# A ring of three PSUM banks for the decays and side pieces of a Mamba stage, and a new layout of those pieces over its slots

## The chip, the cores and the metric

The kernel runs on one NeuronCore of a Trainium2 chip. The core has four engines that take instructions in order from queues of their own: TensorE (PE in the profile; its weight loads are listed as PEld), VectorE (DVE), ScalarE (ACT) and GpSimd (POOL). SyncE (SP) issues DMA transfers. The metric is the time of one execution on the device in microseconds. Three runs of the kernel before gave 2083.98, 2085.44 and 2085.51 us, so the median is 2085.44 us.

## The reference

The input is x of shape (8, 256, 128), which is 2048 tokens of 128 features. Six residual blocks follow each other, each on a layer-normalised x:

```python
x = x + 0.5 * cell(norm(x))        # six small attention nodes
x = x + attention(norm(x))         # 16 heads with rotary positions
x = x + 0.5 * cell(norm(x))
x = x + 0.5 * experts(norm(x))     # top 2 of 8 experts
x = x + mixer(norm(x))             # bidirectional Mamba and an FFT branch
x = x + 0.5 * experts(norm(x))
```

The change lies in the mixer and in the two expert blocks that share its stage. The mixer computes, for each batch entry with 256 channels `d`, 16 states `n` and 256 steps `l`:

```python
u     = silu(causal_conv(x_half))                 # once forward, once reversed
delta = softplus(W_dt @ dt + bias)
h[l]  = exp(delta[l] * A) * h[l-1] + delta[l] * B[l] * u[l]   # per (d, n)
y     = sum_n h[l] * C[l] + D * u
out   = (y_forward + y_reversed) * silu(z)
f     = abs(ifft2(silu(conv(fft2(x_half))))) * max(silu(z))   # then whitened
result = (out + (f - mean) / sqrt(var + 1e-5)) @ W_out
```

The factor `exp(delta * A)` is called the decay below. The reversed direction runs the scan from the last token to the first.

## The kernel before

The 2048 tokens are cut into 4 chunks of 512 (two batch entries each). The two cells and the attention come first and are not touched. One function, `experts_and_mixer`, then holds the first expert block, the mixer and the second expert block. Its scan is cut into 32 units per chunk, so 128 units in all. A unit holds 128 partitions and 2 x 512 elements.

**What a unit passes through.** `spread` (L1154) replicates rows over partitions with TensorE: a matmul pair writes `pU` (the factor delta x u, two PSUM banks), and another pair writes `pA` (delta). Each matmul contracts over one strip of 32 rows: the two of `pU` use one half of the four strips, and the two of `pA` of the unit two further on use the other half. ScalarE turns `pA` into the decay tile `dA` with two Exp instructions (L1177). `feed` (L1187) multiplies `pU` by B on VectorE in place. `scan` (L1198) is one VectorE instruction, after which GpSimd multiplies the result by C into `hc` (L1200). `sums` (L1211) adds two units' `hc` into the accumulator `py` on TensorE.

**What sets the order.** The code runs under a manual schedule of TensorE, VectorE, ScalarE and GpSimd: each of these queues keeps the order in which the program names the instructions. A loop over slots i issues scan(i), feed(i+1), the pieces listed for that slot in `before`, sums(i-3) in odd slots, the pieces listed in `after` (`last=True`), and last spread(i+2, i+4). A spread therefore makes `pU` two slots ahead and the decay four slots ahead. Slot s of chunk c is i = 32c + s; in a chunk's slots work of three chunks stands side by side.

**The pieces.** All that is not the scan is cut into pieces placed with `at(slot, function, ...)`: the convolutions (`convolve`), the gate, the silu calls, the low-rank step sizes (`ranks`, `steps`, `softplus`, `delta`), the DMA copies of B and C (`rows`), the FFT branch (`frequencies`, `pairs`, `mix`, `mirror`, `halves`, `over_channels`, `folds`, `over_tokens`, `magnitude`, `moments`, `whiten`), and the end (`weigh`, `join`, `output`). Most of the TensorE pieces write one PSUM bank that ScalarE then copies out. `mix` writes two SBUF tiles, `mix0` and `mix1`, which `mirror` reads on GpSimd in three instructions; there is one buffer of each.

**PSUM.** Of the eight banks, `pU` holds a ring of two tiles of two banks (four), `py` holds one, `pA` has one tile of two banks (tag "a"), and all pieces share one bank (tag "p", `bank` at L843). The transposes `pt` of the expert blocks use tag "a".

**Tables.** ScalarE loads a table (`ACT_TABLE_LOAD`) before silu, before Sqrt, and before it goes back to Exp and Ln. In a middle chunk silu runs in slots 20 and 32 and Sqrt in slot 45, so there are six loads per chunk.

Of the kernel before, what the change touches and what calls it, by code (L numbers as in the profile page):

```python
# [10 lines left out]
F32 = mybir.dt.float32  # L11
# [6 lines left out]
P = 128  # L18
# [780 lines left out]
def experts_and_mixer(nc, tc, ident, nhalf, x, cols, ins, w, given, store):  # L799
# [19 lines left out]
    with ExitStack() as ctx:  # L819
# [13 lines left out]
        for i in range(4):  # L833
            c = COLS["Dp"].start + i
            nc.gpsimd.tensor_scalar(w["D"][:, i, :], ident, cols[:, c : c + 1], None, ALU.mult)

        gots = [{} for _ in range(NCH)]
        before, after = {}, {}

# [1 line left out]
            (after if last else before).setdefault(slot, []).append(lambda: f(*a))  # L841

        def bank(shape):  # L843
            return ps.tile(shape, F32, tag="p", bufs=1, name="p")

# [85 lines left out]
        class Experts:  # L933
# [58 lines left out]
            def turn(self, n):  # L992
                if not 0 <= n < NCH * NT:
                    return
                both = self.tiles[n]["both"]
                pt = ps.tile([P, 4, P], F32, tag="a", bufs=1, name="pt")
                for k in range(4):
                    nc.tensor.transpose(pt[:, k, :], both[:, 0, k, :], ident)
                nc.scalar.copy(both[:, 1], pt)
# [71 lines left out]
        def exponentials():  # L1071

            nc.scalar.preload_act_table_set("natural_log_exp_and_others")
# [73 lines left out]
        def unit(n):  # L1147
            s = n % UNITS
            return n // UNITS, s // 16, s // 8 % 2, s // 2 % 4, s % 2
# [1 line left out]
        units = [{} for _ in range(NCH * UNITS)]  # L1151
        N = len(units)

        def spread(n, m):  # L1154

            todo = []
            if 0 <= n < N:
                ch, t, r, i, jp = unit(n)
                pU = ps.tile([P, 2, CT], F32, tag="u", name="pU")
                todo.append((pU, gots[ch]["du", t][:, r, :], i, 2 * (1 - jp)))  # L1160
                units[n]["dB"] = pU
            if 0 <= m < N:
                ch, t, r, i, jp = unit(m)
                pA = ps.tile([P, 2, CT], F32, tag="a", bufs=1, name="pA")
                todo.append((pA, gots[ch]["dl", t][:, r, :], i, 2 * jp))
            for jj in range(2):
                for dst, src, i, j in todo:
                    rs = slice(32 * (j + jj), 32 * (j + jj) + 32)
                    nc.tensor.matmul(  # L1169
                        dst[:, jj, :], w["sel"][rs, i, :], src[rs, :], start=True, stop=True  # L1170
                    )
            if 0 <= m < N:
                ch, t, r, i, jp = unit(m)
                dA = pool.tile([P, 2, CT], F32, tag="dA", name="dA", bufs=4)
                for jj in range(2):
                    j = 2 * jp + jj
                    nc.scalar.activation(  # L1177
                        dA[:, jj, :], pA[:, jj, :], AF.Exp, scale=A[:, r, t, i, j : j + 1]
                    )
                units[m]["dA"] = dA  # L1180

        def feed(n):
            if not 0 <= n < N:
# [144 lines left out]
            )  # L1328

        def magnitude(ch):  # L1330
            nc.scalar.activation(gots[ch]["mag"], gots[ch]["mag"], AF.Sqrt)
            exponentials()

        def largest(ch):
            got = gots[ch]
# [58 lines left out]
        def output(ch):  # L1394
            y = gots[ch]["sz"]
            po = bank([P, NT, D])
            for t in range(NT):
                for d in range(2):
                    nc.tensor.matmul(
                        po[:, t, :],  # L1400
                        y[:, d, t * P : (t + 1) * P],
                        w["outT"][:, d, :],
                        start=(d == 0),
                        stop=(d == 1),
                    )
            o = pool.tile([P, NT, D], F32, tag="sq", name="o", bufs=2)
            nc.scalar.copy(o, po)
            nc.gpsimd.tensor_tensor(x[ch], x[ch], o, ALU.add)

        def u_of(ch, t):  # L1410
            return lambda: (gots[ch]["u", t], None)
# [8 lines left out]
        def prepare(experts, c, k, *room):  # L1420

            at(k, experts.statistics, c)
            at(k + 1, experts.scale, c, *room)
            at(k + 1, experts.transpose, c, last=True)
            at(k + 2, experts.logits, c, last=True)
            at(k + 3, experts.gates, c, last=True)
# [31 lines left out]
        for n in range(NCH * NT + 2):  # L1458
            at(end + 1 + n, second.step, n)
        prepare(second, 2, end + 3, room)  # L1460
        prepare(second, 3, end + 8)

        at(-27, fetch, None)
        at(-27, fetch, 2)
# [13 lines left out]
        at(0, conv_weights, 3, 0, last=True)  # L1478
        at(1, conv_weights, 3, 1, last=True)

        for ch in range(NCH):

            o = (ch - 1) * UNITS
            if ch == 0:
                at(-8, ranks, ch, 1)
                at(-8, largest, ch)
                at(-7, steps, ch, 0, 0)
                at(-6, steps, ch, 0, 1)
                at(-6, exponentials)
                at(-6, softplus, ch)  # L1490
            else:
                for part, k in enumerate((-3, -2, 0, 0)):
                    at(o + k, normalize, ch, part)
                at(o + 1, features, ch)
                at(o + 2, convolve, ch, 1, 0)
                at(o + 12, convolve, ch, 1, 1)
                at(o + 16, convolve, ch, 0, 0)
                at(o + 17, gate, ch, 0, last=True)
                at(o + 18, convolve, ch, 0, 1)
                at(o + 19, gate, ch, 1, last=True)  # L1500
                at(o + 20, silu, u_of(ch, 0), u_of(ch, 1), sz_of(ch), sc_of(ch - 1, 0))
                at(o + 20, exponentials)
                at(o + 21, largest, ch)
                at(o + 21, ranks, ch, 0, last=True)
                at(o + 22, ranks, ch, 1)
                at(o + 23, steps, ch, 0, 0)
                at(o + 23, steps, ch, 0, 1, last=True)
                at(o + 24, softplus, ch)
            at(o + 24, rows, ch, 0, 0)
            at(o + (26 if ch == 0 else 25), delta, ch, 0, 0)  # L1510
            at(o + 26, delta, ch, 0, 1)
            at(o + 26, rows, ch, 0, 1)
            v = o + 4 * (ch == 0)
            at(v + 28, steps, ch, 1, 0)
            at(v + 29, steps, ch, 1, 1)
            at(v + 30, softplus, ch)
            at(v + 31, delta, ch, 1, 0)
            at(o + 32, rows, ch, 1, 0)
            at(v + 32, delta, ch, 1, 1)
            at(o + 34, rows, ch, 1, 1)  # L1520
            o += UNITS
            for t in range(2):
                at(o + 16 * t + 3, skip, ch, t, 0)
                at(o + 16 * t + 4, skip, ch, t, 1)
                at(o + 16 * t + 18, weigh, ch, t)
            at(o - (2 if ch == 0 else 1), frequencies, ch, 0)
            at(o - 1, frequencies, ch, 1, last=True)
            at(o + 10, pairs, ch, 1)
            at(o + 11, pairs, ch, 2)

            final = ch + 1 == NCH
            mixes = (12, 14, 16, 18) if final else (14, 24, 26, 29)
            for co, k in enumerate(mixes):
                at(o + k, mix, ch, co, 0, last=True)
                at(o + k + 1, mix, ch, co, 1, last=True)
                at(o + k + 2, mirror, ch, co)
            k = o + (21 if final else 32)
            at(k, silu, *(sc_of(ch, co) for co in range(0 if final else 1, 4)))
            at(k, exponentials)
            at(k + 1, halves, ch, 0)  # L1540
            at(k + 2, halves, ch, 1)
            for i in range(4):
                at(k + 3 + i, over_channels, ch, i // 2, i % 2, last=True)
                at(k + 5 + i, folds, ch, i // 2, i % 2)
            for i, j in enumerate((7, 8, 10, 11)):
                at(k + j, over_tokens, ch, i // 2, i % 2, last=True)
            at(k + 13, magnitude, ch)
            if final:
                k -= 3
            at(k + 14 + 3 * final, moments, ch, 0)  # L1550
            at(k + 15 + 2 * final, moments, ch, 1)
            at(k + 17 + final, whiten, ch, 0)
            at(k + 17 + final, whiten, ch, 1)
            at(k + 18 + final, join, ch)
            at(k + 21 - final, output, ch)
        engines = mybir.EngineType
        order = {engines.PE, engines.DVE, engines.Activation, engines.Pool}
        with tc.manual_schedule(engines=order):
            for i in range(min(before), max(*before, *after) + 1):
                scan(i)  # L1560
                feed(i + 1)
                for f in before.get(i, ()):
                    f()
                if i % 2:
                    sums(i - 3)
                for f in after.get(i, ()):
                    f()
                spread(i + 2, i + 4)


SHAPES = {
# [263 lines left out]
```

## Time and profile before

| what | us |
|---|---|
| median of three runs | 2085.44 |
| the profiled execution | 2090.59 |
| its span | 2088.8 |
| first matmul of the first expert block | 1330.1 |
| first unit's scan starts | 1433.5 |
| last unit's scan ends | 2013.4 |
| chunk 0, scan start to scan start | 147.8 |
| chunk 1 | 144.3 |
| chunk 2 | 142.0 |
| chunk 3, to the start of the last scan | 143.5 |
| after the last scan | 75.4 |
| one scan on VectorE | 2.29 |
| one feed on VectorE | 1.21 |
| one product by C on GpSimd | 2.36 |
| one decay Exp on ScalarE (two to a unit) | 0.68 |
| one table load on ScalarE | 1.28 |

Over the whole span TensorE is busy for 93%, VectorE for 75%, ScalarE for 55% and GpSimd for 39%. These are averages over stages with different limits. A timeline row gives the start, the duration, the engine, the line, the operation, the tiles (written <- read), the shapes and a count; the bracket behind it is the time that the engine was idle before it, and who ended that. The time from one scan to the next is that of a slot: 2.29 + 1.21 and a gap of about 0.04 give 3.54 us when nothing else is in the way, and 128 such slots would take 453 us.

### The profile page before, as it was taken

To read this page: it belongs to the slowest core of one execution; us is meant where nothing else is said; L and a number is where in the kernel's file an instruction comes from. 1 tells how busy PE (TensorE), PEld (TensorE's weight loads), DVE (VectorE), ACT (ScalarE), POOL (GpSimd) and SP (SyncE) were. 2 spreads that over 40 slices of the span, in tenths; PEclk is the share of its full clock that TensorE was granted. 3 is DMA by queue.
4 is the path that set the end of the run, shared out by engine and by line. 5 is a ranking of instruction groups with operands and counts; after the bars stand their busy time and mean duration, and the time that the engine had idled before them with its cause. 6 is when DMAs were issued, how large, how long until landed. Compare 5 with 4: busy or idle time off the path is not lost. (4 is left out here: it accounts for less than half of the span.)

```text
span 2088.8 us, 45123 instructions
## 1 busy us (share of the span) xinstructions
PE 1946.3 (93%) x17792; PEld 1127.5 (54%) x17792; DVE 1564.9 (75%) x2669; ACT 1151.7 (55%) x2202; POOL 812.7 (39%) x918
## 2 busy tenths in 40 slices
PE   6999999997999999999999998798888989889888
PEld 4666666654565665666666665453234433334445
DVE  5777777776878767677777777546987978888774
ACT  4777777752333323477777774445355555654544
POOL 3000001026666655100000003443767868778863
PEclk9999999998999999899999999899898999989899
DMA  4000000000000000000000000221000010010000
GB/s 143 3 3 3 3 3 3 3 2 1 2 2 2 2 2 2 2 3 3 3 3 3 3 3 2 107 68 24 11 21 21 1 24 18 4 38 1 1 1 21
DMA packets 21239, 29.23 MB, mean 14 GB/s; under 512 B 12506, under 2 KB 13914, under 8 KB 20260
## 3 DMA queue, kind: packets, MB, share of 16 engines
q1 hardware_dynamic: 20740, 26.15, 4.2%
q8 instruction: 141, 2.31, 0.5%
q14 instruction: 70, 0.57, 0.1%
q10 hardware_dynamic: 288, 0.20, 0.0%
HBM read 16.10 MB, written 1.05 MB: 8 GB/s over the span
## 5 line engine op out<-in xcount | busy, mean ns | idle before, releaser
L344 DVE TENSOR_REDUCE negmax<-sc 128x2 f32<-128x512 f32 x768 | 490.9, 682 | 158.0 <-PE sc L338 157.6
L349 ACT ACTIVATE ex<-sc 128x512 f32<-128x512 f32 x768 | 421.3, 609 | 198.2 <-PE sc L338 197.9
L338 PE MATMUL sc<-qk,qk 32*128 32x256 f32 x6144 | 472.8, 406 | 9.3 <-DVE negmax L344 8.5
L338 PEld LDWEIGHTS sc<-qk,qk 32*128 32x128 f32 x6144 | 296.5, 186 | 146.2 <-ACT ex L349 100.9
L1200 POOL TENSOR_TENSOR hc<-h,C 128x1024 f32<-128x1024 f32 x128 | 301.3, 2359 | 129.1 <-DVE h L1198 118.4
L1198 DVE TENSOR_TENSOR_SCAN h<-dA,pU 128x1024 f32<-128x1024 f32 x128 | 292.2, 2283 | 14.5 <-POOL hc L1200 2.2
L299 ACT ACTIVATE qk<-pp,w_bqk,head_rows 128x256 f32<-128x256 f32 x384 | 197.6, 573 | 74.3 <-PE pp L419 34.7
L85 POOL TENSOR_SCALAR ln_ve<-ln_mv 128x2 f32<-128x2 f32 (+1 forms) x56 | 13.3, 238 | 559.3 <-DVE ln_mv L83 552.0
L1177 ACT ACTIVATE dA<-pA,cols 128x512 f32<-128x512 f32 x256 | 162.1, 684 | 105.1 <-PE pA L1169 102.9
L1187 DVE TENSOR_TENSOR pU<-pU,B 128x1024 f32<-128x1024 f32 x128 | 155.7, 1216 | 76.5 <-PE pA L1169 72.4
L377 PE MATMUL pc<-ex,va 128*32 128x256 f32 x3072 | 206.0, 386 | 0.2 <-DVE y L442 0.2
L1169 PE MATMUL pU<-du,s_sel 32*128 32x512 f32 x512 | 173.2, 690 | 19.4 <-DVE h L1198 18.8
L621 ACT ACTIVATE ex<-sc 128x512 f32<-128x512 f32 x128 | 66.1, 602 | 204.8 <-PE sc L606 204.8
L1169 PE MATMUL pA<-dl,s_sel 32*128 32x512 f32 x512 | 159.3, 698 | 6.3 <-ACT dA L1177 6.3
L606 PE MATMUL sc<-rot,rot 32*128 32x256 f32 x2048 | 136.9, 392 | 1.9 <-POOL rot L589 1.9
L377 PEld LDWEIGHTS pc<-ex,va 128*32 128x32 f32 x3072 | 80.7, 109 | 96.6 <-issue 61.9
L606 PEld LDWEIGHTS sc<-rot,rot 32*128 32x128 f32 x2048 | 99.0, 186 | 37.1 <-issue 23.1
L198 POOL TENSOR_SCALAR w_bqk<-pb,head_rows 128x2 f32<-128x2 f32 x12 | 3.5, 316 | 295.8 <-DVE pb L195 288.9
L624 POOL TENSOR_TENSOR both<-ex 128x512 f32<-128x512 f32 x64 | 80.0, 1273 | 71.3 <-ACT ex L621 71.3
L1169 PEld LDWEIGHTS pU<-du,s_sel 32*128 32x128 f32 x512 | 49.3, 198 | 100.2 <-issue 81.5
L616 DVE TENSOR_REDUCE anegmax<-sc 128x2 f32<-128x512 f32 x128 | 79.5, 685 | 26.7 <-PE sc L606 26.7
L985 DVE TENSOR_TENSOR hid<-ph,gate 128x1024 f32<-128x1024 f32 x32 | 39.1, 1222 | 71.7 <-PE ph L980 68.7
(291 smaller groups left out, 3210.8 us busy)
## 6 DMA issues: line engine op xcount, KB each, us to landing
qk<-turned SPq DMA_DIRECT2D x768, 1.0 KB
s_fft<-s_fft SPq DMA_DIRECT2D x5, 1024.0 KB
du<-ab SPq DMA_DIRECT2D x16, 256.0 KB
B<-low SPq DMA_DIRECT2D x64, 32.0 KB
C<-low SPq DMA_DIRECT2D x64, 32.0 KB
x<-x SPq DMA_DIRECT2D x4, 256.0 KB
s_inK<-s_inK SPq DMA_DIRECT2D x1, 1024.0 KB
out<-x SPq DMA_DIRECT2D x4, 256.0 KB
```

The source lines that it names most:

```text
L299: nc.scalar.activation(t[:, g, :], pp, AF.Identity, scale=w["mask"][:, g : g + 1], bias=w["bqk"][:, c, i, g : g + 1],)
L338: nc.tensor.matmul(sc[:, t, :], lhs[:, t * P : (t + 1) * P], rhs, start=True, stop=True)
L344: nc.vector.tensor_reduce(sh[:, :, 4 * g + j], sc, AX.X, ALU.max, negate=True)
L349: nc.scalar.activation(ex, sc, AF.Exp, scale=FD**-0.5)
L377: nc.tensor.matmul(st["pc"][32 * j : 32 * j + 32, g, :], st[2][:, kt, 2 * j + g, :], st["ex", g, j][:, kt, :], start=(kt == 0), stop=(kt = ...
L606: nc.tensor.matmul(sc[j][:, t, :], lhs[r, part, t * P : (t + 1) * P] if part < 2 else sel[r, :], rhs[r, part, :] if part < 2 else st["nm"] ...
L624: nc.gpsimd.tensor_tensor(both, ex[:, :, 0], ex[:, :, 1], ALU.add)
L1169: nc.tensor.matmul(dst[:, jj, :], w["sel"][rs, i, :], src[rs, :], start=True, stop=True)
L1177: nc.scalar.activation(dA[:, jj, :], pA[:, jj, :], AF.Exp, scale=A[:, r, t, i, j : j + 1])
L1187: nc.vector.tensor_tensor(dB, dB, bcast(gots[ch]["B", r], 2), ALU.mult)
L1198: nc.vector.tensor_tensor_scan(hf, af, bf, 0.0, ALU.mult, ALU.add)
L1200: nc.gpsimd.tensor_tensor(hc, h, bcast(gots[ch]["C", r], 2), ALU.mult)
```

## The change

All of it lies in `experts_and_mixer`.

- **PSUM.** Tag "a" is gone. `bank` becomes a ring of three single banks, from which the pieces, the transposes `pt` and the decays are allocated in program order. A unit's decay takes two of these banks, one for each half, instead of one tile of two.
- **`spread(n, *ms)`** makes one `pU` and the decays of none, one or two units. Its matmuls are issued in the order pU half 0, first decay half 0, pU half 1, first decay half 1, second decay half 0, second decay half 1.
- **Bursts.** Seven slots (12, 26, 44, 58, 76, 90 and 114 of 0 to 127), those in which the silu calls now stand, are marked. The spread of such a slot b makes no decay, nor does that of b+1; those of b+2, b+3 and b+4 make two, one and two.
- **`magnitude`** takes the root as exp(log(x + 1e-30) / 2), two ScalarE passes, with no table load of its own.
- **`output`** is split: the addition to x is a piece `add` with a slot of its own.
- **The layout.** The slots of nearly all pieces change. Silu goes to slots 12 (u and z) and 26 (the FFT branch), convolutions and gates to slots 2 to 10, `ranks` and `steps` to 15 to 17, the `mix` pieces of chunks 0 to 2 to 13, 14, 18 and 20 to 24, their `over_channels` to 30 to 33, and in chunks 0 and 1 `over_tokens` to 36, 37, 43 and 44 (slots 4, 5, 11 and 12 of the next chunk) and `magnitude` to 51 (slot 19 of the next). In the last chunk the FFT branch ends in slot 129 instead of 132. The preparation of the fourth chunk for the second expert block starts three slots earlier.

The diff, cut to its core:

```diff
+        tiny = pool.tile([P, 1], F32, name="tiny")
+        nc.gpsimd.memset(tiny, 1e-30)
...
         def bank(shape):
-            return ps.tile(shape, F32, tag="p", bufs=1, name="p")
+            return ps.tile(shape, F32, tag="p", bufs=3, name="p")
...
-                pt = ps.tile([P, 4, P], F32, tag="a", bufs=1, name="pt")
+                pt = bank([P, 4, P])
...
-        def spread(n, m):
+        def spread(n, *ms):
             todo = []
             if 0 <= n < N:
                 ch, t, r, i, jp = unit(n)
                 pU = ps.tile([P, 2, CT], F32, tag="u", name="pU")
-                todo.append((pU, gots[ch]["du", t][:, r, :], i, 2 * (1 - jp)))
+                for jj in range(2):
+                    todo.append((jj, pU[:, jj, :], gots[ch]["du", t][:, r, :], i, 2 * (1 - jp) + jj))
                 units[n]["dB"] = pU
-            if 0 <= m < N:
-                ch, t, r, i, jp = unit(m)
-                pA = ps.tile([P, 2, CT], F32, tag="a", bufs=1, name="pA")
-                todo.append((pA, gots[ch]["dl", t][:, r, :], i, 2 * jp))
...
+            ms = [m for m in ms if 0 <= m < N]
+            decays = []
+            for k, m in enumerate(ms):
                 ch, t, r, i, jp = unit(m)
                 dA = pool.tile([P, 2, CT], F32, tag="dA", name="dA", bufs=4)
+                units[m]["dA"] = dA
                 for jj in range(2):
+                    pA = bank([P, CT])
+                    todo.append((2 * k + jj, pA, gots[ch]["dl", t][:, r, :], i, 2 * jp + jj))
+                    decays.append((dA[:, jj, :], pA, A[:, r, t, i, 2 * jp + jj : 2 * jp + jj + 1]))
+            for _, dst, src, i, j in sorted(todo, key=lambda v: v[0]):
+                rs = slice(32 * j, 32 * j + 32)
+                nc.tensor.matmul(dst, w["sel"][rs, i, :], src[rs, :], start=True, stop=True)
+            for dA, pA, rate in decays:
+                nc.scalar.activation(dA, pA, AF.Exp, scale=rate)
...
         def magnitude(ch):
-            nc.scalar.activation(gots[ch]["mag"], gots[ch]["mag"], AF.Sqrt)
-            exponentials()
+            mag = gots[ch]["mag"]
+            nc.scalar.activation(mag, mag, AF.Ln, bias=tiny)
+            nc.scalar.activation(mag, mag, AF.Exp, scale=0.5)
...
-                at(o + 12, convolve, ch, 1, 1)
-                at(o + 16, convolve, ch, 0, 0)
-                at(o + 17, gate, ch, 0, last=True)
-                at(o + 18, convolve, ch, 0, 1)
-                at(o + 19, gate, ch, 1, last=True)
-                at(o + 20, silu, u_of(ch, 0), u_of(ch, 1), sz_of(ch), sc_of(ch - 1, 0))
+                at(o + 6, convolve, ch, 1, 1)
+                at(o + 7, gate, ch, 0)
+                at(o + 8, convolve, ch, 0, 0)
+                at(o + 9, gate, ch, 1)
+                at(o + 10, convolve, ch, 0, 1)
+                at(o + 12, silu, u_of(ch, 1), u_of(ch, 0), sz_of(ch))
...
-            mixes = (12, 14, 16, 18) if final else (14, 24, 26, 29)
-            for co, k in enumerate(mixes):
-                at(o + k, mix, ch, co, 0, last=True)
-                at(o + k + 1, mix, ch, co, 1, last=True)
-                at(o + k + 2, mirror, ch, co)
-            k = o + (21 if final else 32)
-            at(k, silu, *(sc_of(ch, co) for co in range(0 if final else 1, 4)))
+            mixes = (6, 8, 10, 11, 12, 13, 14, 15) if final else (13, 14, 18, 20, 21, 22, 23, 24)
+            for k, v in enumerate(mixes):
+                at(o + v, mix, ch, k // 2, k % 2, last=True)
+                if k % 2:
+                    at(o + v + 1, mirror, ch, k // 2)
+            k = o + (18 if final else 26)
+            bursts.add(k)
+            if not final:
+                bursts.add(o + 12)
+            at(k, silu, *(sc_of(ch, co) for co in range(4)))
...
-                spread(i + 2, i + 4)
+                more = 0
+                if i >= -4:
+                    more = next(((0, 0, 2, 1, 2)[i - b] for b in bursts if 0 <= i - b < 5), 1)
+                spread(i + 2, *range(m, m + more))
+                m += more
```

## The prediction

> **What bounds the kernel now.** I looked first at the busy time by stretch, for the four chunks of the scan.
>
> ```profile
> core 0: us, PE busy (x) PEld busy (x) DVE busy (x) ACT busy (x) POOL busy (x), PEclk, DMA share, GB/s
> 1433.50:1581.30 147.80, 127.75 (x548) 46.23 (x546) 122.37 (x82) 70.59 (x112) 92.41 (x64) 0.87 0.06 13
> 1581.30:1725.60 144.30, 130.48 (x620) 55.51 (x616) 120.42 (x87) 81.00 (x126) 111.91 (x86) 0.93 0.06 15
> 1725.60:1867.60 142.00, 129.02 (x616) 55.40 (x616) 118.93 (x80) 80.73 (x126) 109.22 (x78) 0.94 0.07 16
> 1867.60:2011.10 143.50, 123.40 (x608) 58.31 (x604) 115.86 (x111) 68.43 (x111) 117.76 (x90) 0.89 0.03 6
> ```
>
> VectorE works about 120 us of each 142 to 148, so a chunk can lose 22 to 25 us at most. But TensorE shows 123 to 130 us, at a granted clock of 0.87 to 0.94. The two are near balance, and any TensorE work that is added can become the limit. Next I read what VectorE waits for.
>
> ```profile
> its engine sat idle before it (us, times) until:
>   PE pA L1169: 72.4, 44
> ```
>
> These waits stand before feed: the `pU` it needs comes late, because TensorE stands in its own queue. The timeline around slot 52 (silu) shows why.
>
> ```profile
> 1667.41 1.28 ACT L1079 ACT_TABLE_LOAD   x1
> 1668.71 2.01 ACT L1079 ACTIVATE u<-u 128x1024 f32<-128x1024 f32 x2
> 1670.62 1.04 ACT L1079 ACTIVATE sz<-sz 128x1024 f32<-128x1024 f32 x1
> 1671.56 0.71 ACT L1081 ACTIVATE fsc<-fsc,cols 128x512 f32<-128x512 f32 x1
> 1672.27 1.28 ACT L1073 ACT_TABLE_LOAD   x1
> 1673.57 1.27 ACT L1177 ACTIVATE dA<-pA,cols 128x512 f32<-128x512 f32 x2
> 1675.36 3.73 PE L1091 MATMUL p<-u,s_xproj 128*96 128x512 f32 x4 [3.81 <-ACT o L1407]
> 1681.04 1.23 DVE L1187 TENSOR_TENSOR pU<-pU,B 128x1024 f32<-128x1024 f32 x1 [5.74 <-PE pA L1169]
> ```
>
> ScalarE is in silu and its two table loads for 6.1 us. The one piece bank waits for its copy behind that, `ranks` waits for the bank, and the next `pU` stands behind `ranks`. TensorE idles 3.81 us, comes back at half clock (four passes take 3.73 us instead of 1.9), and VectorE loses 5.74 us.
>
> **What goes.** I added VectorE's idle times from its timeline, by place, over the 128 slots (gaps over 0.15 us; chunks 0 to 3):
> - Silu at slots 20 to 25: 5.5 + 7.6 + 4.8 = 17.9. Silu at slots 32 to 38: 6.6 + 6.1 + 4.5 = 17.2. In the new layout TensorE has no decay in the silu slot and the next, and what it does there needs banks last read before silu. I count 35 as gone.
> - Slots 28 to 30: 6.5 + 4.5 + 6.7 = 17.7. `steps` waits for the DMA that still reads `ab` (1.24 us at 1709) and its two pieces share a bank. That DMA moves from slot 26 to 20, nine slots ahead: gone.
> - Slots 0 and 1: 3.27 + 5.05, TensorE's filter pieces behind the bank. `steps` leaves: 7 gone.
> - Root and GpSimd pieces at 46, 78, 109 and 110: 1.1 + 1.1 + 3.2 = 5.4, gone; two loads of 1.28 against one more pass of 1.06.
> - Convolutions at 17 to 20: 4.0; they move, and are counted below.
> - Slots 114 to 126, with the second expert block's transposes: 16.2. They wait for normalised tiles as before. I count half, 8.
>
> Sum 77.
>
> **What comes: TensorE in the bursts.** The prices are in these rows:
>
> ```profile
> 2008.46 1.13 PE L1169 MATMUL pU<-du,s_sel 32*128 32x512 f32 x4
> 2009.52 1.06 PE L762 MATMUL p<-m_gate,exT 128*128 128x8 f32 x8
> 1469.10:1475.90 6.80, 5.98 (x24) 1.26 (x24) 6.54 (x5) 1.32 (x3) 5.48 (x3) 0.50 0.22 57
> ```
>
> The first is a spread of `pU` alone: the queue moves on after 1.06 us, as much as with a decay beside it (1741.93 to 1743.00). Leaving a decay out saves TensorE nothing. Doing it later costs: four strips run at once, and a second decay needs strips again. In b+2 the fourth half needs the bank of the first: 1.11 us of matmul, 0.09 to the Exp, 0.68, 0.05 back, 1.06 of its own, 3.0 in all. In b+3 decay and `pU` are of opposite parity and share strips: 2.1. In b+4 both happen: 4.05. A burst takes 2.1 + 3.0 + 2.1 + 4.05 = 11.3 us against 5 x 1.06 = 5.3, so 6 us more; seven bursts are 42 us. No row shows a spread with two decays. Its bounds are 1.06 (all beside the other) and 4.2 (all in series); I take the chain, since its links are rows.
>
> What of it lies on the path I read by stretch of slots, full-clock row prices: convolution 3.5, `mix` 2.3, `over_*` 1.9, `ranks` 1.75, `steps` and `gate` 0.95, `skip` 0.96, `output` 2.0, `features` 0.55, `sums` 1.0. VectorE's side is 3.54 a slot plus its extras.
> - Slots 28 to 31: TensorE 2.0 + 1.9 + 3.8 + 2.0 + spreads 10.2 = 19.9; VectorE 14.2 + 2.5 = 16.7.
> - Slots 0 to 11 of the next chunk: 9.5 + 0.55 + 14 + 1.9 + 1.9 + 6 + 12.6 = 46.4; VectorE 43.2.
> - Slots 12 to 17: 1.9 + 4.6 + 3.5 + 1.9 + 3 + 12.3 = 27.2; VectorE 21.2.
>
> Over these 22 slots TensorE is 12.4 above, and a `pU` may be 2.2 us late before feed notices (feed and scan, 3.5, less 1.2): 10 us on the path, twice. Chunk 0 adds 2 in slots 12 to 17 (it has no `over_tokens` yet), slots 92 to 95 one, the last burst one: 24. In slots 18 to 27 VectorE has the more (43.7 against 33), so TensorE's excess is hidden there.
>
> **What comes: `mix` behind `mirror`.** A copy into `mix0` must wait for the `mirror` before it, now in the same slot (21 and 23). The row for this in the kernel before is 4.1 us at 1702.60, where slots 58 to 60 cost VectorE 1.1. Now `delta` (2.36 on GpSimd) stands a slot ahead and, from chunk 1 on, `moments` (2.8 of small GpSimd instructions) just before `mirror`: I trace `mirror` done 14.3 us after the start of slot 20, while TensorE wants the bank at 8. The next `mix` is queued there, and the `pU` of slot 24 behind it. VectorE loses 2 in chunk 0, 4 each in chunks 1 and 2, and 3 in chunk 3 (slots 108 to 112): 13. Bounds: 1.1 x 4 = 4, and TensorE's whole wait each time, 6.6 x 4 = 26.
>
> **What comes: the clock.** Half clock was granted from 1469.1 to 1475.9 though TensorE had about 2 us of work in every slot and no idle stretch above 2.40 us. The new slots 25 to 27 look the same (2.0, 3.0, 2.0) just ahead of the heavy slots 28 to 30. I count 2 us in three chunks and 3 in the last: 9. [...]
>
> **Elsewhere.** Ahead of the scan chunk 1's statistics move before the filter folds: 0.9 on VectorE and 1.6 on GpSimd twice, on engines that feed the filters, so +1 (bounds 0 and 3). After the last scan, of the four table loads between 2016 and 2028 three fall away, and two `over_tokens` (3.8 us of TensorE) move ahead; but `whiten` now stands before the second silu on ScalarE and waits for 2.8 us of GpSimd chain, and `output` follows in the third expert step. I take -2 (bounds -8 and +4). The `rows` copies start at most a slot or two off and have five slots or more to their use; `add` and `tiny` are short and off the path. These count as nothing.
>
> **Sum.** -77 + 24 + 13 + 9 + 1 - 2 = -32 in the profiled execution (2090.59), which lies 0.25% above the median. 2090.6 - 32 = 2058.6, less 0.25%, gives 2053.5: I say 2054. 0.2%, or 4 us, is about what a measurement can tell from no change, so "faster" starts at 2081.
>
> **Rivals.**
> - *The ring hides the bursts.* If the fourth half and the strips overlap more than the chain says, TensorE's excess of 24 falls to 4, and with bounds of 4 for `mirror` the sum is -61: 2024. For it: VectorE's floor of 120 a chunk allows it. Against it: TensorE's sums are above VectorE's even with 1.06 a spread.
> - *The bursts run at half clock, slower.* Place: the spreads of b+2 to b+4. At half clock (2.0 a set in 1469.78 to 1471.80) they take 5.1 + 4.1 + 7.1, and with 2.1 for the first two 18.4: 13 above before instead of 6. All seven give +49 on -32: 2102. It decides from 10.6 us a burst. For it: half clock followed silu twice in chunk 1 (1585.1 and 1673.9). Against it: TensorE now has 2 to 4 us of work in b and b+1.
> - *The banks are short in another place, no change.* Decays share banks with pieces, and in slots 17 to 19, 29 and 30 ScalarE has 3.4 to 5.3 us. If TensorE lost 2 us in each over three chunks, 30 of the 32 are gone: 2083. Against it: tracing slots 16 to 19 I find each bank free 0.2 to 1.0 us ahead, and short only in slot 30.
>
> **Chances.** Forecast 0.50 (its own range 2036 to 2081), hidden bursts 0.18, half clock 0.22, banks 0.10 (a third of it to each sign). Faster 0.50 + 0.18 + 0.03 = 0.71, same 0.05, slower 0.24. The range of 8 in 10 goes from the first rival's 2024 to 2100, just short of the second's.
>
> **What the profile after would show.** No feed gap above 2 us in slots 12 to 14 and 26 to 27; feed gaps of 1 to 3 us in slots 14 to 17 and 28 to 31, ended by TensorE; spreads with two decays of 3 and 4 us; a ScalarE wait for `fsc` of about 5 us at slots 53 and 85 with a feed gap of 2 to 5 behind it; four table loads in a middle chunk; chunks of about 138 us. I am wrong if spreads with two decays take 2 us or 6, or if slots 2 to 11 take much over 3.9 each.

## The result, and the profile after

The changed kernel takes 2085.73 us (median of 12 runs, 2082.58 to 2091.85), the kernel before, beside it on the same chip, 2085.74 us (12 runs, 2076.25 to 2092.07). The ratio is 0.9999, with a 95% interval of 0.9984 to 1.0013: no difference that can be measured. The prediction said 2054 us, faster. The profiled execution spans 2086.0 us against 2088.8 before.

The busy time by stretch, for the four chunks of the scan, as it was shown of the kernel before:

```profile
core 0: us, PE busy (x) PEld busy (x) DVE busy (x) ACT busy (x) POOL busy (x), PEclk, DMA share, GB/s
1427.40:1573.50 146.10, 131.72 (x544) 51.83 (x548) 122.92 (x83) 75.78 (x118) 97.57 (x68) 0.89 0.06 14
1573.50:1720.80 147.30, 138.34 (x627) 61.47 (x620) 121.00 (x88) 80.52 (x129) 110.74 (x85) 0.93 0.06 15
1720.80:1871.60 150.80, 141.38 (x611) 61.88 (x613) 119.33 (x79) 78.84 (x123) 109.54 (x78) 0.89 0.07 15
1871.60:2006.30 134.70, 119.29 (x624) 58.89 (x616) 115.13 (x111) 63.07 (x106) 112.87 (x87) 0.97 0.03 6
```

TensorE's busy time is what grew: 530.7 us over the four, 510.6 before. Chunks 1 and 2 became longer (144.3 and 142.0 before), the last one shorter (143.5 before). From the first scan to the start of the last it takes 578.9 us, against 577.6. What lies ahead ends 6.1 us earlier, what follows the last scan takes 2.0 us longer.

VectorE's waits, over the whole span; the columns are total, times, longest:

```profile
engine line waited for: us in total, times, longest us
DVE pU L1188 <- PE p L1179: 77.9, 46, 7.3
DVE pU L1188 <- PE pU L1179: 10.5, 5, 6.3
```

Before the change feed waited 76.2 us in all: the 72.4 us behind the decays' matmul that the prediction shows, and one wait of 3.8 us behind `pU`'s own. Now it waits 88.4 us, of which 6.3 lie ahead of the first scan (3.7 before). The waits stand in other places. I added VectorE's idle times by place again, as in the prediction (us):

| place | before | after |
|---|---|---|
| silu of old slots 20 to 25 and 32 to 38 | 35.1 | 0 |
| old slots 28 to 30 | 17.7 | 0 |
| slots 0 and 1 | 8.3 | 0.1 |
| root, convolutions at the old places | 9.4 | 0 |
| slots 114 to 126 | 16.2 | 9.6 |
| burst of 12: slots 14 to 18 of chunks 0, 1, 2 | - | 7.4, 7.2, 8.8 |
| burst of 26: slots 30 to 32 of chunks 0 and 1, 29 to 32 of chunk 2 | - | 12.7, 3.6, 12.8 |
| convolution and gate, slots 33 to 46 and 66 to 78 | - | 4.4, 4.4 |
| `mix` behind `mirror`, slots 23 to 25 of chunks 0, 1, 2, and slot 112 | - | 2.1, 5.2, 5.9, 1.9 |
| sum | 86.7 | 86.1 |

What should go, went: 77.0 us. Almost the same amount came, 76.4. Not all of it is feed waiting for TensorE: in the 7.2 and the 8.8 us, 1.9 us each are the scan of slots 47 and 79 waiting for GpSimd's product (`hc`).

### The profile page after: what moved, and what is told of

Its sections match the earlier page's. It is cut to its first block, busy times and chain, and to the rows that moved or that the text cites. A ratio compares the mean times of both kernels' runs of the same rounds, so it can differ in the third digit from the quotient of the medians.

```text
span 2086.0 us, 45112 instructions
## 1 busy us (share of the span) xinstructions
PE 1962.5 (94%) x17792; PEld 1143.6 (55%) x17792; DVE 1563.0 (75%) x2669; ACT 1144.8 (55%) x2197; POOL 808.9 (39%) x919
## 5 line engine op out<-in xcount | busy, mean ns | idle before, releaser
L1201 POOL TENSOR_TENSOR hc<-h,C 128x1024 f32<-128x1024 f32 x128 | 301.2, 2356 | 131.0 <-DVE h L1199 88.4
L1181 ACT ACTIVATE dA<-p,cols 128x512 f32<-128x512 f32 x256 | 162.3, 685 | 110.4 <-PE p L1179 107.1
L1179 PE MATMUL pU<-du,s_sel 32*128 32x512 f32 x512 | 154.0, 676 | 16.4 <-DVE h L1199 15.8
L1179 PE MATMUL p<-dl,s_sel 32*128 32x512 f32 x512 | 161.8, 662 | 4.6 <-ACT dA L1181 4.6
L1179 PEld LDWEIGHTS pU<-du,s_sel 32*128 32x128 f32 x512 | 42.2, 195 | 90.5 <-issue 67.1
```

The source lines that it names most:

```text
L1179: nc.tensor.matmul(dst, w["sel"][rs, i, :], src[rs, :], start=True, stop=True)
L1181: nc.scalar.activation(dA, pA, AF.Exp, scale=rate)
L1201: nc.gpsimd.tensor_tensor(hc, h, bcast(gots[ch]["C", r], 2), ALU.mult)
```

## The experiments

All times are medians; each ratio is against runs of the kernel before on the same chip, whose medians were 2086.2 to 2086.4 in the three groups. Two runs add work that nothing reads; they are named. A trace is one execution, so a difference of some us between two traces can be chance: ahead of the scan, nine of these programs are the same, and their first scan starts anywhere from 1424.2 to 1427.7 us. Theory A: the bursts cost the gain. Theory B: something else in the layout does (first the order in which the bank pieces come, then the banks themselves).

### No bursts

```diff
-                    more = next(((0, 0, 2, 1, 2)[i - b] for b in bursts if 0 <= i - b < 5), 1)
+                    more = 1
```

> The changed kernel with one decay in every slot, so the ring and the new layout stay and the bursts go. In the changed kernel VectorE idles 54 us in slots 12 to 18 and 28 to 32 of the four chunks. Theory A (the bursts took the gain: strips shared with pU, the fourth half behind the first's bank, half clock): most of it goes, some 5 us per silu slot come back because decays stand behind silu again, 2050 to 2070. Theory B (the layout of the pieces took the gain, mix behind mirror above all): no change, 2080 to 2090. Theory C (the skipped decays do hide silu, and the bursts pay for themselves): slower, 2095 to 2115.

Measured: 2054.36 us, ratio 0.9842 [0.9824, 0.9861]. Without bursts the kernel is 31 us faster than with them. The same table of stretches:

```profile
1424.20:1558.00 133.80, 120.76 (x564) 47.27 (x564) 123.73 (x82) 77.74 (x123) 97.67 (x68) 0.94 0.06 14
1558.00:1699.90 141.90, 127.72 (x624) 56.17 (x616) 120.71 (x87) 79.27 (x126) 110.55 (x85) 0.93 0.06 15
1699.90:1840.70 140.80, 126.39 (x620) 56.03 (x616) 119.16 (x79) 77.62 (x121) 109.35 (x78) 0.93 0.07 16
1840.70:1974.90 134.20, 113.51 (x608) 55.99 (x600) 114.97 (x111) 62.39 (x105) 114.27 (x88) 0.96 0.03 7
```

TensorE is busy for 488.4 us, 42.3 less than with bursts, for the same arithmetic. In the slots that follow silu, 14 to 18 and 28 to 32 of chunks 0 to 2, VectorE now waits 23.5 us in all (the longest 6.58); the changed kernel loses 52.5 there. So leaving decays out of the silu slots can save at most these 23.5 us, and with the bursts 52.5 are lost there.

### `pU` first in each spread

```diff
-                    todo.append((jj, pU[:, jj, :], gots[ch]["du", t][:, r, :], i, 2 * (1 - jp) + jj))
+                    todo.append((jj - 2, pU[:, jj, :], gots[ch]["du", t][:, r, :], i, 2 * (1 - jp) + jj))
```

> The changed kernel with both halves of pU issued ahead of all decays in each spread. In burst slots feed now starts when a decay half that shares its strip is done, 1 us after pU's own matmuls (1496.72 against 1495.79). Theory A: two such spreads in each of seven bursts, about 1 us each, and any decay that waits for a bank no longer holds pU's second half: 10 to 15 us less, 2070 to 2076. Theory B: within 4 us of 2085.

Measured: 2085.31 us, ratio 1.0004 [0.9986, 1.0021]. No effect. The waits at slots 14, 16 and 18 of chunk 0 became 2.0, 2.2 and 3.1 in place of 2.0, 3.0 and 2.3: what one feed gained, the next lost. The order within a spread does not matter here.

### The ring alone

The kernel before, with `bank` on three banks and the changed kernel's `spread` for one decay; old layout, old root.

```diff
-            return ps.tile(shape, F32, tag="p", bufs=1, name="p")
+            return ps.tile(shape, F32, tag="p", bufs=3, name="p")
...
-                pt = ps.tile([P, 4, P], F32, tag="a", bufs=1, name="pt")
+                pt = bank([P, 4, P])
```

> The kernel before with the ring of three single banks alone: old layout, one decay per slot, Sqrt. Ahead of the scan the changed kernel is 6 us shorter (82.4 against 88.5) and slots 0 and 1 lose 0.1 instead of 8.3; if the ring does that, 2071 to 2079. If it is the moved steps and statistics, 2083 to 2088. If decays and pieces are short of banks in the old silu slots, above 2090.

Measured: 2057.2 us, ratio 0.9854 [0.9836, 0.9872]. The ring by itself brings 29 us; layout and root bring 3 more on top, which the two intervals do not tell from nothing. Part of the 29 I had not seen at all: it comes ahead of the scan. In the profiled execution the scan stage starts at 1423.7, not 1433.5, but not all of these 9.8 us are the ring's. From the first matmul of the first expert block (at 1306.5 us in the kernel before; the table of times has a later one, 1330.1) to the first scan it takes 127.0 us before, 125.3 with the layout alone and 124.0 with the root alone, all three with one bank, and 118.9 with the ring alone and 119.6 in the changed kernel. So the ring is worth some 4 to 8 us there. The filters' pieces ahead of the scan take their bank from the same `bank`, and VectorE waits there behind TensorE, first in the kernel before and then with the ring:

```profile
1356.05 1.22 DVE L985 TENSOR_TENSOR hid<-ph,gate 128x1024 f32<-128x1024 f32 x1 [2.38 <-PE ph L980]
1376.02 1.23 DVE L985 TENSOR_TENSOR hid<-ph,gate 128x1024 f32<-128x1024 f32 x1 [11.44 <-PE ph L980]
1384.13 1.23 DVE L985 TENSOR_TENSOR hid<-ph,gate 128x1024 f32<-128x1024 f32 x1 [4.33 <-PE ph L980]
```

```profile
1351.07 1.23 DVE L985 TENSOR_TENSOR hid<-ph,gate 128x1024 f32<-128x1024 f32 x1 [0.74 <-PE ph L980]
1368.81 1.23 DVE L985 TENSOR_TENSOR hid<-ph,gate 128x1024 f32<-128x1024 f32 x1 [9.23 <-PE ph L980]
1376.19 1.23 DVE L985 TENSOR_TENSOR hid<-ph,gate 128x1024 f32<-128x1024 f32 x1 [3.59 <-PE ph L980]
```

The first and the third of these waits are 2.4 and 4.3 us in the two other runs with one bank as well. The second is 8.5 us in both, so its 11.44 us belong to that one execution, and the ring does not shorten it.

Within the scan stage the ring empties slots 0 and 1 (8.3 to 0.9) and shortens chunks 0 and 3 by 10.8 and 9.5 us. Chunks 1 and 2 do not gain (-2.0 and +0.2).

### The layout alone

New layout and new root, no bursts, and the banks of the kernel before (one for pieces, a pair for decays).

```diff
-            return ps.tile(shape, F32, tag="p", bufs=3, name="p")
+            return ps.tile(shape, F32, tag="p", bufs=1, name="p")
...
-                    more = next(((0, 0, 2, 1, 2)[i - b] for b in bursts if 0 <= i - b < 5), 1)
-                spread(i + 2, *range(m, m + more))
+                    more = 1
+                spread(i + 2, m if more else -1)
```

> The new layout and the new root, with one decay in every slot, and the banks of the kernel before: one bank for pieces and a pair for decays. It completes a square: the ring alone took 29 us (ratio 0.9854), ring, layout and root without bursts 32 us (0.9842). Theory ring: what I put down to the moves and to the root (28 us at slots 28 to 30, 0 and 1, and root) was waits for the one bank, so the layout without the ring is worth nothing: within 8 us of the kernel before, 2078 to 2094. Theory of my prediction's ledger: the DMA that moves from slot 26 to 20, the filters' pieces that leave slots 0 and 1 and the root take away 17.7 + 7 + 5.4 whatever the banks, the mirror gives back 13: 17 us faster, about 2069. Third: two pieces in a slot wait for each other behind silu, and the layout needs the ring: 10 us or more slower than before, 2096 or above.

Measured: 2095.73 us, ratio 1.0044 [1.0025, 1.0062]. Both my ledger (2069) and the first theory (2078 to 2094) fall; the third stands at its edge. Without the ring the new layout loses 9 us. Slots 28 to 30 did become short, as I had said, but new waits stand at slots 14, 18, 23 and 27. This is TensorE and ScalarE at slot 27 of chunk 0:

```profile
1544.35 1.21 PE L1238 MATMUL p<-s_FT,first 128*128 128x278 f32 x4
1551.40 2.22 PE L1238 MATMUL p<-s_FT,first 128*128 128x278 f32 x4 [5.85 <-ACT xe L1241]
```

```profile
1545.79 1.28 ACT L1084 ACT_TABLE_LOAD   x1
1547.08 2.56 ACT L1084 ACTIVATE fsc<-fsc,cols 128x512 f32<-128x512 f32 x4
1549.66 1.28 ACT L1076 ACT_TABLE_LOAD   x1
1550.96 0.39 ACT L1241 COPY xe<-p 128x278 f32<-128x278 f32 x1
```

The second piece of `frequencies` needs the one bank, and its copy stands behind silu on ScalarE: TensorE idles 5.85 us and comes back at about half speed: the same four matmuls take 2.22 us in place of 1.21. So the two parts are not additive: layout with root +9, ring -29, all -32.

### The root alone

> The kernel before with the root as exp(log/2) alone. My ledger had root and GpSimd pieces at 5.4 us of VectorE's waits in slots 46, 78, 109 and 110: 5 us faster, 2079 to 2083. Rival: the two loads lie beside other work, and those waits are for GpSimd's and TensorE's pieces: within 2 us of before.

Measured: 2084.88 us, ratio 0.9991 [0.9980, 1.0002]. The rival: no difference that can be told. Two of the six table loads of a middle chunk are gone, but VectorE's waits at slots 46, 78, 109 and 110 stay (1.1, 1.2, 2.3 and 0.9 us). So the 5 us were not the root's.

### Shorter bursts

Two other patterns in place of 0, 0, 2, 1, 2.

```diff
-                    more = next(((0, 0, 2, 1, 2)[i - b] for b in bursts if 0 <= i - b < 5), 1)
+                    more = next(((0, 2)[i - b] for b in bursts if 0 <= i - b < 2), 1)
```

> The changed kernel with a shorter burst: no decay in the silu slot, two in the next, one in each after it. Theory array: a burst costs what its spreads take TensorE beyond 1.06 us each; here one spread of about 4 us is left of those of 3.0, 2.1 and 4.05, an excess of 3 us in place of 6, so half of the 31 us comes back: about 2070, ratio 0.990 to 0.994. Theory silu: the price is that late decays queue behind silu and its table loads on ScalarE; with both in the very next slot TensorE stands at the banks for them, feed gaps of 4 us or more appear in slots 13, 14 and 27, and nothing comes back: 2082 or more.

Measured: 2061.21 us, ratio 0.9879 [0.9861, 0.9897]. Of the 31 us, 25 come back, more than the half that theory array gave.

```diff
-                    more = next(((0, 0, 2, 1, 2)[i - b] for b in bursts if 0 <= i - b < 5), 1)
+                    more = next(((0, 1, 1, 1, 2)[i - b] for b in bursts if 0 <= i - b < 5), 1)
```

> The changed kernel with bursts of the pattern 0, 1, 1, 1, 2 in place of 0, 0, 2, 1, 2: one decay fewer in the silu slot, made up four slots later, and three single decays at odd lag between, which share strips with pU. By my prices its spreads take 1.06 + 3 x 2.1 + 4.05 = 11.4 us, as much as the 11.3 of the changed kernel, while the pattern 0, 2, which was 25 us faster than the changed kernel, takes 5.1 in two slots. Theory array: the sum of TensorE's time in the burst sets the price, strips shared by single decays included: about the time of the changed kernel, 2080 to 2090. Theory doubles: a price is paid for spreads with two decays, which stand at the ring for an Exp; a single late decay costs nothing that VectorE notices: here one double is left as in the pattern 0, 2, and the time is 2055 to 2068.

Measured: 2080.30 us, ratio 0.9966 [0.9950, 0.9981]. Here too one spread holds two decays, but the price stays: the single late decays, which share strips with `pU`, cost almost as much as the double ones. That is theory array. Spread after spread of the changed kernel's first burst in TensorE's timeline (leaving out rows of one matmul):

```profile
1489.34 2.51 PE L1179 MATMUL p<-dl,s_sel 32*128 32x512 f32 x5
1491.78 1.96 PE L1094 MATMUL p<-u,s_xproj 128*96 128x512 f32 x4
1493.67 1.07 PE L1218 MATMUL py<-hc,s_ysel 128*32 128x512 f32 x8
1494.66 1.13 PE L1179 MATMUL pU<-du,s_sel 32*128 32x512 f32 x4
1495.62 1.03 PE L1179 MATMUL p<-dl,s_sel 32*128 32x512 f32 x4
1496.59 1.96 PE L1094 MATMUL p<-u,s_xproj 128*96 128x512 f32 x4
1498.47 1.13 PE L1179 MATMUL pU<-du,s_sel 32*128 32x512 f32 x4
1499.21 1.25 PE L1179 MATMUL p<-dl,s_sel 32*128 32x512 f32 x6
1501.23 1.12 PE L1179 MATMUL p<-dl,s_sel 32*128 32x512 f32 x2 [0.77 <-ACT dA L1181]
1502.28 1.98 PE L1115 MATMUL p<-low,s_dtT 64*128 64x512 f32 x4
```

The spread of b+3 occupies the queue from 1494.66 to 1496.59, 1.93 us; that of b+4 from 1498.47 to 1502.28, 3.81; that of b+2 began at 1488.79 and ends at 1491.78, 2.99. A burst of the changed kernel takes 2 x 1.06 + 2.99 + 1.93 + 3.81 = 10.85 us, 5.55 above one decay a slot; seven are 39. The pattern 0, 1, 1, 1, 2 takes 1.06 + 3 x 1.92 + 3.81 = 10.6 (1.92 is its own row), seven are 37 above. The pattern 0, 2 takes 1.06 + 3.81 (its double runs from 1619.09 to 1622.90), seven are 19 above. Against no bursts these three cost 31, 26 and 7 us of time. From the pattern 0, 2 to that of the changed kernel, 20 us of TensorE's time cost 24 us. The first 19 cost only 7: there the wait behind silu, which the decay left out does save, pays for the rest (at slots 46 and 47 feed and scan wait 3.1 us in all with the pattern 0, 2 and 5.7 without bursts, at slots 78 and 79 3.1 and 6.6).

### Half clock: the same filler, full and in strips

Both are the changed kernel with five more matmuls of 512 columns in slots 25 to 28 of chunks 0 to 2, which nothing reads: on all 128 rows in the first, on 32 rows in the second.

```diff
+        def filler(full):
+            p = bank([P, 2, S])
+            if full:
+                nc.tensor.matmul(p, w["inT"][:, 0:P], xTm, start=True, stop=True)
+            else:
+                nc.tensor.matmul(p, w["inT"][0:32, 0:P], xTm[0:32], start=True, stop=True)
...
+        for ch in range(3):
+            for r in (25, 26, 27, 27, 28):
+                at(ch * UNITS + r, filler, True)
```

> The changed kernel with five extra matmuls of 128 rows by 512 columns, whose results nobody reads, in slots 25 to 28 of chunks 0 to 2: 0.86 us of TensorE each where VectorE sets the pace. In the changed kernel half clock is granted from 1549.1 to 1569.6 although TensorE is busy without a gap from 1550.9 on, and slots 30 to 32 lose 12.7 us (12.8 in slots 94 to 96, 3.6 in 62 to 64 with full clock). [...] Theory E (it follows whether TensorE is busy): it is not held by more work in slots that have none of the idle time, 2085 to 2092.

> The changed kernel with the same five extra matmuls in slots 25 to 28 of chunks 0 to 2 as in the run with full ones, of the same 512 columns and so about the same time each, but on 32 rows in place of 128; nothing reads them. With full ones half clock in the chunk-0 stretch fell from 20.5 to 10.2 us and the time by 4 us. Theory work: the granted clock follows how much of the array is used, rows times columns, so these do not help: half clock is granted from about 1549 to 1570 as without them, about 20 us, and the time is that of the changed kernel or a little more, 2085 to 2090. Theory busy: the clock follows how long TensorE is busy or how long it stands idle, so strips help as much as full ones: about 10 us of half clock there and 2080 to 2084.

Measured: full rows 2082.39 us, ratio 0.9975 [0.9963, 0.9988]; strips 2092.25 us, ratio 1.0022 [1.0004, 1.0041]. The clock of the stretch in chunk 0, in the changed kernel, with full rows, and with strips (columns as in the table of stretches; PEclk is the sixth number after the comma):

```profile
1549.10:1569.60 20.50, 18.72 (x43) 7.43 (x45) 11.97 (x7) 9.03 (x13) 13.92 (x11) 0.50 0.03 7
```

```profile
1535.70:1549.10 13.40, 13.34 (x62) 5.26 (x62) 13.00 (x16) 9.37 (x15) 10.88 (x11) 1.00 0.05 11
1549.10:1555.70 6.60, 6.60 (x22) 1.98 (x20) 6.33 (x5) 3.12 (x6) 6.27 (x8) 1.00 0.00 0
1555.70:1565.90 10.20, 10.20 (x27) 4.44 (x28) 5.43 (x3) 5.64 (x9) 7.17 (x4) 0.50 0.04 10
```

```profile
1535.70:1551.10 15.40, 14.32 (x71) 5.20 (x69) 14.99 (x17) 9.25 (x14) 12.73 (x15) 1.00 0.03 6
1551.10:1578.40 27.30, 26.53 (x59) 10.28 (x58) 13.25 (x8) 12.47 (x21) 16.02 (x8) 0.50 0.07 15
```

With strips TensorE is busy 14.32 of 15.40 us, its longest idle time there is 0.98 us, and half clock is granted all the same, for 27.3 us. With full rows it is granted 6.6 us later and for 10.2 us, and even that begins when TensorE has been busy for 19.94 of the last 20.0 us: from 1551.51 on it ran the decays of a doubled spread, on strips, and from 1553.95 on matmuls of 64 rows. So in this stretch neither the busy share nor an idle time tells where half clock comes, and full rows help where strips do not. That speaks for theory work and against theories E and busy, as far as one stretch of three traces can: each is one execution, so chance is not excluded, and what decides when half clock comes is not shown.

The price is another matter, and there my estimate failed: from slots 30 to 32 and 94 to 96, which lose 12.7 and 12.8 us where slots 62 to 64 lose 3.6 at full clock, I had 10 to 18 us. In the traces the full filler saves 3.4 us in chunk 0 and nothing in chunks 1 and 2. In chunk 1 the half clock from 1699.3 to 1706.1 is gone, and slots 62 to 64 lose 3.6 us as before; in chunk 2 half clock comes back at the same slots, for 10.2 us in place of 23.9, and later waits for GpSimd take back what that gives. The strips came out slower than either theory said. Their own executions show what the clock is worth: nine at a mean granted clock of 0.958 to 0.962 took 2091.7 to 2098.3 us, three at 0.965 to 0.971 took 2076.5 to 2085.6.

### `mix` a slot behind `mirror`

Without bursts, and with a slot between a `mirror` and the next `mix` into its tile:

```diff
-            mixes = (6, 8, 10, 11, 12, 13, 14, 15) if final else (13, 14, 18, 20, 21, 22, 23, 24)
+            mixes = (6, 8, 10, 11, 12, 13, 14, 15) if final else (13, 14, 18, 19, 21, 22, 24, 25)
...
-                    more = next(((0, 0, 2, 1, 2)[i - b] for b in bursts if 0 <= i - b < 5), 1)
+                    more = 1
```

> One decay in every slot, and in chunks 0 to 2 the pieces of mix at 13, 14, 18, 19, 21, 22, 24, 25 in place of 13, 14, 18, 20, 21, 22, 23, 24, so that a slot lies between a mirror and the next mix into its tile. Theory mirror: the feed gaps at slots 23 to 25 (1.9 in chunk 0, 5.7 and 4.8 in chunks 1 and 2 without bursts) are the wait of mix for mirror; they fall to 1 each and the time is 7 to 10 us less than without the move: 2045 to 2048. Rival: the last mix and mirror now stand at slots 25 and 26, just ahead of silu, over_channels and the filters' statistics, and the wait comes back there: 2052 to 2058.

Measured: 2049.48 us, ratio 0.9816 [0.9797, 0.9836], 5 us less than without the move. The waits at slots 23 to 26 fell to 1.5 us or less a chunk, but those at slot 28, behind silu, grew from 3.1, 3.1 and 3.5 to 4.2, 4.5 and 5.4. So half of the expected gain came, and part of the wait came back as the rival has it. With the pattern 0, 2 the same move is worth more:

> The pattern 0, 2 at all seven bursts together with the moved pieces of mix. If the two gains are apart (25 us and 4.9 us): 2056. If they share a wait: 2060 or more.

Measured: 2050.17 us, ratio 0.9829 [0.9812, 0.9845], 11 us below the pattern 0, 2 without the move, where I had 5.

### Two short bursts with the moved `mix`

Moved `mix`, the pattern 0, 2 only at the silu of slots 44 and 76:

```diff
-            bursts.add(k)
-            if not final:
+            if ch and not final:
                 bursts.add(o + 12)
```

> Moved pieces of mix, and a burst 0, 2 only at the silu of slots 44 and 76; one decay in every other slot. Without bursts feed waits 5.4 and 6.8 us at slots 46 and 78 behind that silu, with the pattern 0, 2 it waits 2.8 in two slots; in chunk 0 and behind the silu of slots 26, 58 and 90 the pattern bought nothing. So 5 to 7 us less than without bursts: 2042 to 2045, the fastest. Rival: the wait that goes at 46 and 78 returns as a queue at slots 47 to 50, 2047 to 2052.

Measured: 2042.73 us, ratio 0.9796 [0.9777, 0.9815], inside the expected range and the lowest median of all. That it beats the moved `mix` alone is not shown: the intervals overlap, and both kernels take either time. Without the two bursts three executions took 2049.3 to 2049.6 us at a mean granted clock of 0.970 and one 2041.7 at 0.973; here three took 2040.8 to 2042.9 at 0.973 and one 2049.5 at 0.969. Of the 7.0 us between the two profiled spans, 3.3 lie ahead of the scan, where the programs are the same. What is shown is that the waits behind silu fall. VectorE at slots 45 to 47 without bursts (moved `mix`), and then here:

```profile
1615.32 2.29 DVE L1199 TENSOR_TENSOR_SCAN h<-dA,pU 128x1024 f32<-128x1024 f32 x1
1623.12 1.23 DVE L1188 TENSOR_TENSOR pU<-pU,B 128x1024 f32<-128x1024 f32 x1 [5.52 <-PE p L1179]
```

```profile
1615.46 1.23 DVE L1188 TENSOR_TENSOR pU<-pU,B 128x1024 f32<-128x1024 f32 x1 [1.14 <-PE p L1179]
1617.67 2.29 DVE L1199 TENSOR_TENSOR_SCAN h<-dA,pU 128x1024 f32<-128x1024 f32 x1 [0.97 <-POOL hc L1201]
1620.92 1.23 DVE L1188 TENSOR_TENSOR pU<-pU,B 128x1024 f32<-128x1024 f32 x1 [0.97 <-PE p L1179]
```

One wait of 5.52 us becomes three of about 1; at slot 78 one of 6.88 becomes three of about 1 as well. From the first scan to the start of the last it takes 537.1 us, against 540.8. Leaving a decay out takes away wait in the two places where silu makes feed wait longer than the 2.75 us that the pattern 0, 2 adds to TensorE.

## Why the prediction was wrong

**What goes: right in size, wrong in cause.** I had 77 us and 77.0 went. But I put much of it down to places: the DMA that moves, the filters' pieces that leave slots 0 and 1, the root. The runs put it elsewhere: the layout alone loses 9 us, the root alone changes nothing that can be measured, the ring alone gains 29. The layout needs the ring; the ring does not need the layout. That the two sums meet so closely is partly luck, and so is that the kernel without bursts takes 2054 us, the number that I forecast for the kernel with them.

**TensorE in the bursts: prices right, cover wrong.** This is the step that failed. The spreads were predicted at 3.0, 2.1 and 4.05 and measured 2.99, 1.93 and 3.81. I had 42 us of TensorE for seven bursts; the spread rows give 39, and busy time is 42.3 higher than without bursts, part of it work stretched by half clock (the granted clock is 0.89 in chunks 0 and 2, and 0.94 and 0.93 there without bursts). What I got wrong is "What of it lies on the path": 24. The table of places has 61.3 for bursts and convolutions together. To part the clock from it I take each place where the clock was full, chunk 1 for slots 30 to 32 (3.6) and, for slots 14 to 18, chunk 0 or what the others show with its slot 18 (2.3) in place of 3.8 and 5.5: 7.4 + 5.6 + 5.6 + 3 x 3.6 + 2 x 4.4 = 38.2. So the path at full clock took some 38, not 24; 3.7 of the 38 are the two waits for GpSimd, which stand in the bursts but are not TensorE's. I summed 22 slots and set TensorE's total against VectorE's, which lets TensorE's light slots pay for heavy ones. They cannot: `pU` has two tiles, and TensorE may not write the next before the scan has read it. In the slots ahead of the burst it stands idle for that:

```profile
1546.77 1.13 PE L1179 MATMUL pU<-du,s_sel 32*128 32x512 f32 x4 [1.82 <-DVE h L1199]
1550.88 1.19 PE L1179 MATMUL pU<-du,s_sel 32*128 32x512 f32 x1 [2.98 <-DVE h L1199]
```

In chunk 0, where I allowed 2 us in slots 12 to 17, VectorE lost 7.4 in slots 14 to 18. Half clock from 1477.4 to 1484.2, right behind silu, has a share in that too, which I did not measure by itself.

**The clock: cause right, size wrong.** I had 9. Of the 61.3, 23 remain after the 38: 9.1 and 9.2 in slots 29 to 32 of chunks 0 and 2, 4.8 at slots 50 and 82. This is worked out from like places of different chunks. Other traces agree, where the same slots met the other clock: with strips, slots 62 to 64 lose 9.7 us at half clock in place of 3.6, and slot 50 2.3 at full clock in place of 3.8; with `pU` first, slots 94 to 96 lose 2.6 at full clock in place of 12.2. Half clock was not longer in all than before, 92.2 us of the scan stage against 105.8; it stood where feed was already late. VectorE in chunk 0:

```profile
1555.53 2.29 DVE L1199 TENSOR_TENSOR_SCAN h<-dA,pU 128x1024 f32<-128x1024 f32 x1
1565.16 1.23 DVE L1188 TENSOR_TENSOR pU<-pU,B 128x1024 f32<-128x1024 f32 x1 [7.34 <-PE p L1179]
1571.20 1.23 DVE L1188 TENSOR_TENSOR pU<-pU,B 128x1024 f32<-128x1024 f32 x1 [2.38 <-PE p L1179]
1578.75 1.23 DVE L1188 TENSOR_TENSOR pU<-pU,B 128x1024 f32<-128x1024 f32 x1 [3.00 <-PE p L1179]
```

The rival "the bursts run at half clock" named this mechanism with 49 us for all seven bursts; the truth lies between it and the forecast, since some bursts met half clock and the others did not. As in the row that the prediction shows, where TensorE idled for 2.40 us at most, half clock came at 1549.1 with no idle time above 2.98 us around it.

**`mix` behind `mirror`: right.** I had 13 and a ScalarE wait with a feed gap of 2 to 5 behind it. ScalarE and VectorE around slot 55:

```profile
1677.03 0.39 ACT L1266 COPY mix<-p 128x270 f32<-128x270 f32 x1 [9.10 <-POOL fsc L1277]
```

```profile
1683.51 1.23 DVE L1188 TENSOR_TENSOR pU<-pU,B 128x1024 f32<-128x1024 f32 x1 [4.30 <-PE p L1179]
```

The places sum to 15.0. Taking the wait away saved 5 and 11 us in the two runs that did: a place's wait is not its price.

**Elsewhere.** Ahead of the scan I had +1 and -6.1 came; I put the ring at nothing there, and it is worth 4 to 8. After the last scan I had -2 and +2.0 came. **The sum:** -77 + 38 + 23 + 15 - 6 + 2 = -5, against -2.8 in the spans; 0.8 of the rest is VectorE's own work, which takes 478.4 us in place of 477.6 in the scan stage, and 1.4 are waits in slots 4, 103 and 108 that the table leaves out. One reading was off, without weight in the sum: by the rows shown a chunk can lose 23 to 28 us, not 22 to 25 (143.5 less 115.9 in the last). **Of the signs that I named**, feed gaps in slots 14 to 17 and 28 to 31 ended by TensorE, spreads of 3 and 4 us and the wait for `fsc` came; chunks of 138 us did not, and "spreads with two decays take 2 us or 6", which would have proved me wrong, was the wrong place to look.

## What to carry to other kernels

When work is moved out of a slot to be done in later ones, price not only what it costs there but what the later engine has free in each slot: with two tiles between the engines, a light slot cannot pay for a heavy one, and a sum over twenty slots hides the loss. A change of several parts is best seen as a square: here the ring alone was worth 29 us, the layout alone cost 9, and the third part, the bursts, meant to help both, took all of it back; each part by itself took one run to see. And work that ran side by side need not do so when it comes later: here `pU` and a decay on strips of their own took 1.06 us together, and a spread with a decay that came a slot late and shared `pU`'s strips took 1.93.

## What was not expected of the hardware

In the stretch that the fillers changed, the granted clock did not go by how busy TensorE was. With a filler on strips of 32 rows TensorE was busy for 14.32 of 15.40 us with no idle time above 0.98 us, and half clock was granted for the next 27.3 us; with the same number of columns on 128 rows half clock came 6.6 us later than without a filler, and lasted 10.2 us. So a stretch with many matmuls on strips looked busy to the profile here and was followed by half clock all the same. What decides when half clock comes, these runs do not settle.
